# The late part of a four-layer kernel: written order or scheduler's order

## The chip, the cores and the metric

One core of a Trainium2 chip runs the whole program in one launch. Times are device microseconds (us) of an execution. The kernel before was run three times; one more execution was taken with the hardware profiler. A core has five engines that each work through a queue of their own, in the order in which the queue was built: TensorE (PE, with weight loads listed apart as PEld), VectorE (DVE), ScalarE (ACT), GpSimd (POOL) and SyncE (SP, which here only issues DMAs). They wait for each other through semaphores.

## The reference, cut to what matters

Two images of 256 channels and 32 x 32 points pass four residual layers. Layers 0 and 1 are attention over the points; layer 2 is windowed attention and a mixture of experts; layer 3 is additive attention and a mixture of experts. The change concerns what follows layer 2's attention:

```python
t = t + _L2_ffn_ref(_ln_t(t), ...)
t = t + _L3_attn_ref(_ln_t(t), ...)
t = t + _L3_ffn_ref(_ln_t(t), ...)

# _L2_ffn_ref: 8 experts, hidden width 1024; each token uses the best two
h = gelu(einsum('end,edh->enh', xe, W1) + b1)
y = einsum('enh,ehd->end', h, W2) + b2
out = (weights[:, :, None] * sel).sum(axis=1)

# _L3_attn_ref: U = 32 units, a tanh for each pair of points and unit
h = tanh(q[:, :, None, :] + k[:, None, :, :] + bh)
e = einsum('biju,u->bij', h, Wa[:, 0]) + ba[0]
v = einsum('bij,bjd->bid', softmax(e), inputs)

# _L3_ffn_ref: 8 experts, hidden width 512; each token uses the best two
```

All data are float32.

## The kernel before, in words

**The stages.** The late part is a class of generators, one for each stage and image, and each `yield` ends a piece. For an image `b` and a layer `l` (2 or 3):

- `dispatch` (L976 to L1006) normalizes the tokens (`norm`, L939 to L950; `channels`, L952 to L961, turns them by TensorE), chooses experts (`route`), writes each token's row to two places of a table in memory by 16 indirect DMAs of GpSimd (L989), and adds the second bias (transpose, copy to `wT` L1000, matmul L1002).
- `experts` (L1124 to L1226) works through 23 tiles of 128 rows. A tile's weights come by two indirect DMAs on GpSimd's queue (L1140, `up` and `down`, three buffers each), its rows by a DMA on SyncE's (`xr`, L1150). Two transposes turn the rows (L1158). Then follow up matmuls (L1183, two pieces of 8 per tile in layer 2 and one in layer 3), bias on VectorE (L1188), gelu on ScalarE (L1172), down matmuls (L1197, 8 per tile in layer 2 and 4 in layer 3), a copy, and a store on SyncE's queue.
- `collect` (L1228 to L1262) gathers two rows for each token by 16 indirect DMAs (L1241) and adds them, weighted, on VectorE (L1254). For layer 2 it goes on with the norm and with `project` (L1284 to L1307); for layer 3 with `finish` (L1264 to L1280), which writes the output.
- `additive` (L1309 to L1390) is layer 3's attention of one image, in 64 steps. In a step ScalarE makes four tanh tiles of 128 x 1024 (`th`, L1322, eight buffers). A step later `products` puts eight matmuls on TensorE, which pick and sum the units: two halves of 512 keys, and in each half one matmul for every tanh tile, which goes to its own 32 rows of the result, so to its own column group of TensorE:

```python
for a in range(2):
    for c, h in enumerate(tanhs[s]):
        nc.tensor.matmul(
            pe[i][c * U : (c + 1) * U, a, :], lhsT=self.pick[:, k, :], rhs=h[:, a, :],
            start=(k == 0), stop=(k == G - 1),
        )
```

  Eight steps fill one accumulator of 128 x 1024 (`ps_e`, a pool with one buffer, L1331); VectorE copies it out and takes its maximum (L1338). Exponentials (L1349), a turn (L1361) and the values' matmuls (L1368) follow as extra jobs between later steps.

In the profile a matmul of the program shows as two records of TensorE[...]: 1024 products are 2048 records of L1331.

**What sets the order.** `run` (L1393 to L1420) holds a plan: each generator has a start and an end on a common scale and a number of pieces. A heap always advances the generator whose next piece comes first. So the pieces of image 0's attention and of image 1's layer-2 experts alternate, and those of image 1's attention and image 0's layer-3 experts. The program is built in this merged order. In the kernel before, the loop stands inside `with self.tc.manual_schedule():`, under which each engine's queue has its instructions in the order in which the program builds them. Without it, a scheduler places each instruction among those that it takes to be ready, and the order of building gives the priority. Both apply when the program is built, not when it runs.

The pools that limit how far work can run ahead: three buffers each for up weights, down weights and `xr`; two accumulators for the up matmuls; one each for the down matmuls, the turned rows and `ps_e`; two shared by everything else.

Of the kernel before, what the change touches and what calls it, by code (L numbers as in the profile page):

```python
# [858 lines left out]
class Late:  # L859
# [531 lines left out]
    def run(self):  # L1391
        psum = lambda name, bufs: self.ctx.enter_context(self.tc.tile_pool(name=name, bufs=bufs, space=PSUM))
        p_m = psum("lt_m", 2)  # L1393
        self.sb = self.ctx.enter_context(self.tc.tile_pool(name="late_sb", bufs=2))
        self.misc = lambda shape, name: p_m.tile(shape, F32, name=name, tag="ps_m")
        self.p_x, self.p_h, self.p_y, self.p_e = psum("lt_x", 1), psum("lt_h", 2), psum("lt_y", 1), psum("lt_e", 1)

        plan = [
            (self.experts(2, 0), 0, 185, 72),
            (self.dispatch(2, 1), 5, 165, 48),  # L1400
            (self.collect(2, 0), 186, 225, 18),
            (self.experts(2, 1), 186, 480, 72),
            (self.additive(0), 226, 535, 65),
            (self.collect(2, 1), 482, 525, 18),
            (self.additive(1), 536, 850, 65),
            (self.dispatch(3, 0), 546, 622, 40),
            (self.experts(3, 0), 625, 790, 50),
            (self.collect(3, 0), 795, 840, 11),
            (self.dispatch(3, 1), 880, 900, 40),
            (self.experts(3, 1), 905, 1000, 50),  # L1410
            (self.collect(3, 1), 1001, 1040, 11),
        ]
        heap = [(start, k) for k, (_, start, _, _) in enumerate(plan)]
        with self.tc.manual_schedule():
            while heap:
                heap.sort()
                at, k = heap.pop(0)
                step, start, end, pieces = plan[k]
                if next(step, False) is None:
                    heap.append((at + (end - start) / pieces, k))  # L1420


@with_exitstack
# [72 lines left out]
```

## Time and profile before

| | |
|---|---|
| three runs | 3246.14, 3235.66, 3243.29 us |
| median | 3243.29 us |
| profiled execution: its time | 3233.88 us |
| its span | 3232.2 us |
| its mean granted TensorE clock | 0.943 of full |
| instructions | 71102 |
| busy: PE, PEld, DVE, ACT, POOL | 2927.0, 1890.0, 1886.4, 2000.8, 390.9 us |

Stages of the late part in the trace, in us from the span's start:

| event | at |
|---|---|
| layer 2's experts, image 0: first turn, last down | 2024.2, 2258.5 |
| additive attention, image 0: first product, last product | 2325.6, 2668.8 |
| layer 2's experts, image 1: last down | 2594.6 |
| additive attention, image 1: first product, last product | 2680.2, 3005.1 |
| layer 3's experts, image 0: first up, last down | 2771.1, 2942.7 |
| layer 3's experts, image 1: first scatter, first up, last down | 3049.5, 3099.6, 3198.7 |
| end | 3232.2 |

How to read the page: the busy share of an engine is a mean over stages with different limits, so the slices (40 equal parts of the span) and windows of single stretches say more. In a group's row, the first number after the bar is its busy time, the next the mean of one in ns; behind the second bar stands the idle time of the engine just before these instructions, with what ended most of it. In a timeline row stand the start, the length, the engine and line, the operation, how many records, and in brackets the idle time before and its releaser.

### The profile page before, as it was taken

What the parts mean: (1) busy time and instruction counts of PE and PEld (TensorE: products, weight loads), DVE (VectorE), ACT (ScalarE), POOL (GpSimd) and SP (SyncE); (2) the same over time, 40 slices, a digit from 0 to 9 for tenths busy, and PEclk for the clock granted to TensorE, in tenths of its full rate; (3) what the DMA queues carried; (4) which work ended last, traced back from release to release, by engine and by line L of the source; (5) the groups of instructions that cost most, each with busy time, mean ns of one, the idle gap of its engine ahead of it and who ended that gap; (6) DMA issues with size and microseconds to landing.
All of it is one profiled execution on the core that took longest, in us unless ns stands there. A gap on an engine that the chain in (4) does not pass through costs nothing. (4 is left out here: it accounts for less than half of the span.)

```text
span 3232.2 us, 71102 instructions
## 1 busy us (share of the span) xinstructions
PE 2927.0 (91%) x29260; PEld 1890.0 (58%) x29260; DVE 1886.4 (58%) x3668; ACT 2000.8 (62%) x2990; POOL 390.9 (12%) x544
## 2 busy tenths in 40 slices
PE   7999999999999998999999788888699988999565
PEld 4566666666666665566676565776566633564355
DVE  5998898989898986354454574532422243222423
ACT  1887887878788875565566231111399878979200
POOL 3000000000000000000000002232311011322043
PEclk9999999999999998999999887899799998999688
DMA  3000000000000001000000100765554310543066
GB/s 119 3 3 3 3 3 3 3 3 3 3 3 3 3 3 28 1 1 1 1 2 2 24 1 27 269 232 205 208 182 172 134 30 19 175 147 95 19 229 198
DMA packets 175859, 206.85 MB, mean 64 GB/s; under 512 B 118368, under 2 KB 144880, under 8 KB 163760
## 3 DMA queue, kind: packets, MB, share of 16 engines
q0 software_dynamic: 34848, 167.82, 14.8%
q1 hardware_dynamic: 139248, 34.04, 4.8%
q8 instruction: 230, 3.77, 0.5%
q14 instruction: 93, 0.76, 0.1%
q10 hardware_dynamic: 1440, 0.47, 0.1%
HBM read 172.97 MB, written 28.57 MB: 62 GB/s over the span
## 5 line engine op out<-in xcount | busy, mean ns | idle before, releaser
L314 ACT ACTIVATE sc<-sc,sa_shift 128x1024 f32<-128x1024 f32 x512 | 585.1, 1148 | 53.5 <-DMA sa_shift<-sa_min 53.4
L1322 ACT ACTIVATE th<-kT,qb 128x1024 f32<-128x1024 f32 x512 | 541.0, 1134 | 73.7 <-PE ps_e L1331 58.3
L277 PE MATMUL ps_s<-kT,qT 64*32 64x512 f32 x8192 | 504.4, 596 | 9.0 <-ACT sc L287 8.7
L353 PE MATMUL ps_o<-wt,v 128*64 128x128 f32 x6144 | 503.4, 276 | 0.0
L353 PEld LDWEIGHTS ps_o<-wt,v 128*64 128x64 f32 x6144 | 442.2, 137 | 42.6 <-issue 42.6
L327 DVE STREAM_TRANSPOSE wt<-sc 128x768 f32<-128x768 f32 x512 | 465.7, 943 | 1.0 <-ACT sc L314 1.0
L287 ACT COPY sc<-ps_s 128x1024 f32<-128x1024 f32 x256 | 257.4, 1006 | 115.9 <-PE ps_s L277 42.7
L1172 ACT ACTIVATE h<-hb 128x512 f32<-128x512 f32 x138 | 86.1, 624 | 388.0 <-DVE hb L1188 333.8
L1183 PEld LDWEIGHTS ps_h<-xe,ew 128*128 128x128 f32 x2208 | 275.3, 201 | 79.3 <-issue 56.6
L1183 PE MATMUL ps_h<-xe,ew 128*128 128x128 f32 x2208 | 289.9, 288 | 30.4 <-DMA ew<-in_l_up,rt_rows 28.0
L298 DVE TENSOR_REDUCE sa_least<-sc 128x1 f32<-128x1024 f32 x256 | 306.1, 1196 | 1.9 <-ACT sc L287 1.9
L284 DVE TENSOR_SCALAR_CACHE_REDUCE sc<-ps_s 128x1024 f32<-128x1024 f32 x256 | 301.3, 1177 | 5.9 <-PE ps_s L277 5.9
L1331 PE MATMUL ps_e<-th,pick 128*32 128x512 f32 x2048 | 295.2, 616 | 1.4 <-DVE sc_a L1338 1.4
L1197 PE MATMUL ps_y<-ew,h 128*128 128x256 f32 x1104 | 260.6, 386 | 3.9 <-ACT h L1172 2.7
L1188 DVE TENSOR_TENSOR hb<-ps_h,ew 128x512 f32<-128x512 f32 x138 | 95.3, 691 | 280.8 <-PE ps_h L1183 239.2
L154 DVE TENSOR_SCALAR_CACHE_REDUCE sc<-ps_s 128x1024 f32<-128x1024 f32 x128 | 151.8, 1223 | 179.3 <-PE ps_s L148 179.3
L353 PE MATMUL ps_o<-wl,v_odd 128*64 128x128 f32 x2048 | 252.1, 277 | 0.0
L277 PEld LDWEIGHTS ps_s<-kT,qT 64*32 64x32 f32 x8192 | 126.9, 106 | 200.8 <-issue 171.4
L1197 PEld LDWEIGHTS ps_y<-ew,h 128*128 128x128 f32 x1104 | 204.5, 192 | 59.8 <-issue 20.5
L335 PEld LDWEIGHTS ps_t<-ident,sc 128*128 128x128 f32 x1024 | 107.5, 141 | 216.1 <-issue 169.1
L353 PEld LDWEIGHTS ps_o<-wl,v_odd 128*64 128x64 f32 x2048 | 221.3, 137 | 0.0
L335 PE MATMUL ps_t<-ident,sc 128*128 128x128 f32 x1024 | 168.5, 287 | 4.8 <-ACT wl L336 4.1
(269 smaller groups left out, 3607.1 us busy)
## 6 DMA issues: line engine op xcount, KB each, us to landing
xr<-slots_in SPq DMA_DIRECT2D x92, 128.0 KB
slots_out<-y SPq DMA_DIRECT2D x92, 128.0 KB
sa_got<-sa_least SPq DMA_DIRECT2D x512, 0.5 KB
sa_shift<-sa_min SPq DMA_DIRECT2D x512, 0.2 KB
slots_in<-zero POOLq DMA_DIRECT2D x46, 128.0 KB
sa_sums<-sa_total SPq DMA_DIRECT2D x256, 1.0 KB
xT<-in_x SPq DMA_DIRECT2D x4, 496.0 KB
sb_l_w_in<-in_l_w_in SPq DMA_DIRECT2D x1, 1536.0 KB
```

The lines of the kernel that those rows point to most:

```text
L277: nc.tensor.matmul(ps[r][S * c : S * (c + 1), a, :].rearrange("p (b i) -> p b i", i=S), lhsT=qT[half, p, S * i : S * (i + 1)], rhs=keys[ha ...
L284: nc.vector.tensor_scalar(scores[m][0], flat[0], 1.0, None, ALU.mult, ALU.min, accum_out=least[m // 2][:, 0, h : h + 1])
L287: nc.scalar.copy(scores[m][1], flat[1])
L298: nc.vector.tensor_reduce(least[m // 2][:, 1, h : h + 1], scores[m][1], AX.X, ALU.min)
L314: nc.scalar.activation(scores[m][r], scores[m][r], AF.Exp, bias=shift[m // 2][:, r : r + 1], scale=-1.0, accum_out=total[i][:, 2 * p + r, ...
L327: nc.vector.transpose(weights[i, h][:, 2 * p + r, :], scores[m][r][:, :DIRECT])
L335: nc.tensor.transpose(ps[:, g, r, :], s[:, at : at + P], self.ident)
L353: nc.tensor.matmul(sums[i][64 * k : 64 * (k + 1)], lhsT=values, rhs=w, start=(h == 0 and j == 0 and t == 0), stop=(h == 1 and j == 1 and t ...
L1183: nc.tensor.matmul(ps[:, j, :], lhsT=a[:, c, at : at + P], rhs=x[:, c, :], start=(c == 0), stop=(c == CC - 1),)
L1197: nc.tensor.matmul(ps, lhsT=h[:, j, :], rhs=w2[:, j, :], start=(j == 0), stop=(j == HB - 1))
L1322: nc.scalar.activation(h, keys, AF.Tanh, bias=self.qb[b][:, s // G, g : g + 1])
L1331: nc.tensor.matmul(pe[i][c * U : (c + 1) * U, a, :], lhsT=self.pick[:, k, :], rhs=h[:, a, :], start=(k == 0), stop=(k == G - 1),)
```

## The change

The heap loop of `run` leaves the `with` block. The plan, the merged order of building and all stages stay as they are. Layers 0 and 1, whose attention has its own fixed order, are not touched. The whole diff:

```diff
@@ -1411,13 +1411,12 @@
             (self.collect(3, 1), 1001, 1040, 11),
         ]
         heap = [(start, k) for k, (_, start, _, _) in enumerate(plan)]
-        with self.tc.manual_schedule():
-            while heap:
-                heap.sort()
-                at, k = heap.pop(0)
-                step, start, end, pieces = plan[k]
-                if next(step, False) is None:
-                    heap.append((at + (end - start) / pieces, k))
+        while heap:
+            heap.sort()
+            at, k = heap.pop(0)
+            step, start, end, pieces = plan[k]
+            if next(step, False) is None:
+                heap.append((at + (end - start) / pieces, k))
```

Both programs have the same instructions with the same tiles. What differs is their order on the queues: of TensorE's instructions some 8,000 stand elsewhere, of VectorE's some 3,000 rows are involved, and on GpSimd's queue the scatters, gathers and weight fetches are merged in another way.

## The prediction

> **What bounds the kernel now.** I read the slices of the page first, then the windows of the late part (from 2024 us on; the change reaches nothing before it), then the groups, then the order on TensorE and GpSimd inside the stretches that looked full or idle.
>
> ```profile
> PE   7999999999999998999999788888699988999565
> ACT  1887887878788875565566231111399878979200
> PEclk9999999999999998999999887899799998999688
> ```
>
> A slice is 80.8 us. The late part is slices 26 to 40: first TensorE with little ScalarE (image 0's experts), then both full (additive attention beside experts), then a thin tail. The windows put numbers on it: start and end, length, then busy time of PE, weight load, DVE, ACT, POOL, granted clock, DMA share, GB/s.
>
> ```profile
> 2024.00:2260.00 236.00, 198.82 (x1226) 177.25 (x1226) 95.65 (x288) 33.11 (x50) 58.78 (x61) 0.92 0.66 238
> 2260.00:2326.00 66.00, 38.16 (x190) 30.98 (x194) 32.77 (x95) 9.85 (x12) 25.77 (x27) 0.74 0.54 193
> 2380.00:2420.00 40.00, 40.00 (x288) 26.14 (x277) 8.57 (x17) 37.50 (x40) 5.68 (x6) 1.00 0.50 179
> 3005.00:3100.00 95.00, 33.23 (x108) 21.45 (x107) 33.35 (x135) 2.78 (x4) 21.34 (x22) 0.56 0.13 46
> 3100.00:3199.00 99.00, 90.27 (x594) 81.42 (x592) 33.38 (x67) 14.49 (x23) 37.87 (x40) 0.99 0.84 283
> ```
>
> Three kinds of stretch: TensorE with holes (rows 1 and 2: 37 and 28 us idle), TensorE without any (row 3, a sample of 2326 to 2595, where it is busy 268.3 of 269 us), and a tail that waits for scatters (row 4) and then for weights (row 5). In the full stretch ScalarE, which makes the tanhs, is the one that waits, and for the products:
>
> ```profile
> L1322 ACT ACTIVATE th<-kT,qb 128x1024 f32<-128x1024 f32 x512 | 541.0, 1134 | 73.7 <-PE ps_e L1331 58.3
> L1331 PE MATMUL ps_e<-th,pick 128*32 128x512 f32 x2048 | 295.2, 616 | 1.4 <-DVE sc_a L1338 1.4
> ```
>
> So each microsecond added to TensorE between 2326 and 2595 lengthens the kernel by one. TensorE's timeline shows how cheap the products are there:
>
> ```profile
> 2399.55 0.38 PE L1158 MATMUL ps_x<-ident,xr 128*128 128x128 f32 x2
> 2399.86 1.92 PE L1331 MATMUL ps_e<-th,pick 128*32 128x512 f32 x16
> 2401.72 2.05 PE L1183 MATMUL ps_h<-xe,ew 128*128 128x128 f32 x16
> 2403.70 1.93 PE L1331 MATMUL ps_e<-th,pick 128*32 128x512 f32 x16
> ```
>
> A step's eight products (two records each) go to four column groups of 32 and take 1.86 us to the next start. Records of one column group start 0.43 us apart (2399.863, 2400.317, 2400.746, 2401.175), four of them in a row; the other three groups run beside it. Side by side, a product costs 0.23 us; by itself its two records need 2 x 0.43 = 0.86 us before a full-width matmul can follow.
>
> **What the Trainium skill says.** "TensorEngine Tiling (Array Packing)", Key Properties: tiles work independently and in parallel, and a change of tiling mode drains TensorE. The trace agrees with the first (four column groups in the time of one) and doesn't contradict the second: a full matmul starts 0.53 us after the last product record, 0.10 us beyond its 0.43. "DMA: Bandwidth & Descriptors", Two DMAs through the same engine are not ordered: order comes from waiting on the first one's completion. Here each scatter waits for the landing of the one before: in the tail 16 scatters stand 2.67 us apart. "TensorE: Matmul & The Clock Gate", What's actually happening: after an idle window (about 3.4 us) the clock is halved until TensorE has been busy again. The trace agrees: 16 up records take 3.61 us after a hole of 7.34 us and 1.95 us right after.
>
> **The change part by part.** No operation is added or removed. In the built kernel I compared the order on each engine's queue, which executes in order. What moves:
>
> *1. The products are broken up.* Before, all 1024 products stand in unbroken groups of eight or more: 58 runs for image 0, 47 for image 1. After, the scheduler places single products between up and down matmuls, as soon as one tanh is there: 110 runs for image 0 (32 of one, 10 of two, 11 of three, 25 of five, 25 of eight, others) and 91 for image 1. I cost a run at 0.86 us times the products in its fullest column group, plus 0.13 us to leave it and 0.2 us for the extra change of matmul group (an estimate: trace starts of 0.53 against 0.43, and 0.1 to 0.2 where up and down change). A step split 1, 1, 1, 5 costs 0.86 x (1+1+1+2) + 4 x 0.33 = 5.6 us against 2.05. Bounds: streaming alone, 45.6 us for image 0 and 34.4 for image 1 (155.7 and 144.5 against 110.1 each); with 0.6 us instead of 0.33 for each of 52 and 44 extra runs, 77 and 61. Summed along the queue with measured durations (up 0.222 us, down 0.444, turn of x 0.155 per program matmul), first product of image 0 to the last down of image 1's layer-2 experts goes from 272.1 us (trace: 269) to 329.2: **+57**. For image 1 beside layer 3's experts, step 20 to the last down goes from 166.5 (trace 168.3) to 191.9: +25. The rest of image 1's splits lies where ScalarE sets the pace (541.0 us / 512 x 4 = 4.2 us of tanh per step) and is hidden; if not, another 20. On the same queue the first turn of image 0's layer-3 experts stands at product step 17 instead of 19, in front of products that it holds up while the scatters are still running: +5. Sum for image 1: **+30**.
>
> *2. Image 0's layer-2 experts (row 1).* GpSimd's queue (first fence) and TensorE's (second) show the hole; brackets hold the idle time before and what ended it:
>
> ```profile
> 2152.51 1.01 POOL L989 DMA_INDIRECT slots_in<-u,rt_slot  x1 [0.30 <-issue]
> 2160.74 0.99 POOL L989 DMA_INDIRECT slots_in<-u,rt_slot  x1 [7.22 <-DMA slots_in<-u,rt_slot]
> 2162.03 0.99 POOL L1140 DMA_INDIRECT ew<-in_l_down,rt_rows  x1 [0.30 <-issue]
> 2163.33 0.97 POOL L1140 DMA_INDIRECT ew<-in_l_up,rt_rows  x1 [0.30 <-issue]
> ```
>
> ```profile
> 2160.12 3.61 PE L1183 MATMUL ps_h<-xe,ew 128*128 128x128 f32 x16 [7.34 <-DMA ew<-in_l_up,rt_rows]
> ...
> 2171.88 2.02 PE L1183 MATMUL ps_h<-xe,ew 128*128 128x128 f32 x16 [2.69 <-DMA ew<-in_l_up,rt_rows]
> ...
> 2183.20 2.02 PE L1183 MATMUL ps_h<-xe,ew 128*128 128x128 f32 x11 [3.83 <-DMA ew<-in_l_up,rt_rows]
> ```
>
> Scatters for image 1 stand in pairs; the second waits some 7 us for the first, which lands behind two weight fetches, and the next fetches stand behind it. After, scatters and fetches alternate one by one and up goes ahead of down. Waits that can go: for weights 7.3 + 2.7 + 3.8 + 2.3 (two short ones), about 7.5 for the copy of wT ahead of the bias matmul (L1000/L1002, now with up matmuls between), 5.1 for the norm, 1.7 of halved clock: 30. Late next is the weight traffic itself (238 GB/s here, 283 at most seen), so I take three quarters: **-22**, bounds -8 and -33.
>
> *3. The seam (row 2).* Image 1's first up weights stand behind the gathers of collect; TensorE waits 9.8 us for them and 4.8 to 5.5 us three times for norm and turn. After, three fetches of each kind stand before the gathers and four expert tiles before the first product. Of 28 idle us I take **-16** (-8 to -24): collect's own chain of gather, add, norm remains.
>
> *4. The end of image 0's attention.* ScalarE is busy 53 of the 74 us between 2595 and 2669 and the products wait with it for norm and values; norms of both halves move ahead: **-7** (0 to -12).
>
> *5. The tail (rows 4 and 5).* Norm of half 0 of image 1 goes earlier on VectorE, beside the last attention steps: -7.5 of the 44 us before the first scatter. On GpSimd's queue three weight fetches of each kind move ahead of most scatters: they hold the scatters up by about 5, and the first up starts some 3 sooner after the last scatter: +2. Six of 46 fetches are then done when the 99 us stretch begins, whose PE sum is 89: -7.5. On SP's queue the loads of x and the stores of y go with their tiles; no hole of TensorE over 3.7 us ended with them before, so I cost that at nothing, and at 3 us where a load comes late. Sum **-13** (0 to -20). If the cover is gone (norm lands late), it is 0.
>
> Sum: +57 + 30 - 22 - 16 - 7 - 13 = **+29 us** on a span of 3232.2, whose run took 3233.9: 3263. The median of the runs shown, 3243.3, lies 9.4 us above that run; with it 3272. I state 3270.
>
> **The rivals.**
> *The scheduler is right (faster).* One mechanism: TensorE's holes of the late part, 58 us in parts 2 to 5, are filled, and the broken products cost only where their streaming can't hide. For it: the holes are in the profile, and the order names early work for each. Against: in the full stretch nothing hides them, ScalarE already waits. It decides where the broken groups cost under 58 us in all; if a single product takes about 0.6 us instead of 1.19, steps cost half as much more, 87 becomes about 40, and with the holes at 65 the time is 3243 - 25 = 3218.
> *Balance.* Splits at streaming cost alone in the two full stretches, about 60, against 58: 3243.
> *A blocked queue (much slower).* TensorE runs in order; a turn or up placed early in front of ready products waits for scatters or weights. For it: layer 3's first turn stands two steps earlier. With another 40 us of such waits (one tail's worth of 16 scatters at 2.67 us): 3310.
> *The change does nothing* is excluded by the orders, which differ on every queue but ScalarE's, nearly.
>
> **How the numbers follow.** Forecast 0.51 (own range 3255 to 3300), much slower 0.12, balance 0.12, faster 0.25. The measurement can tell about 0.3%, 10 us, from no change; so slower 0.63, same 0.12, faster 0.25. The range 3215 to 3315 leaves out about the lower half of the faster case and a part of the slowest.
>
> **What would show it.** Right: between the first product of image 0 and the last down of image 1's layer-2 experts some 320 us instead of 269, TensorE still full, ScalarE's wait for ps_e well above 58 us, timeline rows of L1331 with x2 records and 0.9 us or more to the next start; the first product near 2288 (2326 less 16 and 22); PE waits for up weights around 2160 gone. Wrong: a lone product that costs 0.5 us or less, or a full stretch under 290 us; or holes of over 5 us in it, for weights, scatters or x, which would be the blocked queue.

## The result, and the profile after

| | before | after |
|---|---|---|
| median (13 runs each) | 3237.79 us | 3250.66 us |
| range | 3232.78 to 3247.16 us | 3243.73 to 3260.64 us |
| span of the profiled execution | 3232.2 us | 3247.5 us |

The ratio is 1.0038, with a 95% interval of [1.0025, 1.0051]: the change costs 0.4%, some 13 us by the medians and 15.3 us by the spans. The forecast had the right sign and its range held the time, but its size, +29 us on the span, was about twice what came. The time that it stated, 3270 us, also rested on the median of three runs of the kernel before, 3243.3; thirteen runs give 3237.8, so 5.5 of the 19 us by which it lies too high come from there.

Behind the small sum stand two large ones. First the slices of the page after:

```profile
PE   7999999999999998999999778998999988999756
ACT  2887888878887884565565321111678878678300
PEclk9999999999999998999999877899999999999778
```

The late part again begins with slice 26. ScalarE is fuller earlier there (the attention starts sooner) and emptier beside the experts. The windows, with the columns as in the prediction, for the same five stages:

```profile
2032.00:2224.00 192.00, 185.78 (x1221) 169.71 (x1222) 83.74 (x249) 33.12 (x50) 63.72 (x66) 0.96 0.89 320
2224.00:2276.00 52.00, 37.06 (x212) 29.65 (x210) 30.03 (x94) 6.38 (x10) 21.93 (x23) 0.87 0.63 212
2380.00:2420.00 40.00, 40.00 (x225) 19.54 (x225) 7.46 (x15) 29.14 (x31) 3.79 (x4) 1.00 0.44 149
3035.00:3125.00 90.00, 30.53 (x104) 20.09 (x103) 24.54 (x104) 2.78 (x4) 21.41 (x22) 0.56 0.19 66
3125.00:3213.00 88.00, 87.34 (x595) 81.98 (x596) 32.60 (x67) 14.48 (x23) 37.94 (x40) 0.98 0.88 303
```

Row 1: image 0's experts take 192 us with TensorE busy for 186; the long holes are gone, the mean granted clock is 0.96 instead of 0.92, and the transfers run at 320 GB/s. Row 3: TensorE is as full as before, but gets through 225 records in 40 us where it got through 288, and ScalarE is busy 29 of 40 us. The groups name the waiting:

```profile
L1322 ACT ACTIVATE th<-kT,qb 128x1024 f32<-128x1024 f32 x512 | 543.0, 1135 | 147.0 <-PE ps_e L1331 135.7
L1331 PE MATMUL ps_e<-th,pick 128*32 128x512 f32 x2048 | 386.1, 608 | 21.0 <-DVE ir_y L935 11.4
```

The same 2048 records of products take 386.1 us of TensorE's time instead of 295.2 although one lasts no longer (608 ns against 616): they overlap less. ScalarE's wait for them is 135.7 us instead of 58.3. TensorE's timeline after shows why:

```profile
2362.99 1.05 PE L1331 MATMUL ps_e<-th,pick 128*32 128x512 f32 x4
2363.97 1.38 PE L1183 MATMUL ps_h<-xe,ew 128*128 128x128 f32 x10
2365.28 1.04 PE L1331 MATMUL ps_e<-th,pick 128*32 128x512 f32 x2
2366.26 0.44 PE L1158 MATMUL ps_x<-ident,xr 128*128 128x128 f32 x2
2366.53 0.83 PE L1183 MATMUL ps_h<-xe,ew 128*128 128x128 f32 x6
2367.30 1.90 PE L1331 MATMUL ps_e<-th,pick 128*32 128x512 f32 x10
```

One product (two records) holds TensorE for 0.98 us until the next start, two products 0.98, five 1.83, eight 1.85. A step in pieces of two, one and five pays 0.98 + 0.98 + 1.83 = 3.79 us where it paid 1.85.

Added up between image 0's first product and the last down of image 1's layer-2 experts, records of products hold TensorE for 145.0 us instead of 95.0, over 103 separate runs instead of 51. The expert matmuls hold it 5.3 us longer, although 26 fewer of their records stand there. Together that is the 55 us by which this stretch grows.

### The profile page after: what moved, and what is told of

Read it like the earlier page. It is cut to its first block, busy times and chain, and to the rows that moved or that the text cites. A ratio compares the mean times of both kernels' runs of the same rounds, so it can differ in the third digit from the quotient of the medians.

```text
span 3247.5 us, 71067 instructions
## 1 busy us (share of the span) xinstructions
PE 2999.5 (92%) x29260; PEld 1886.3 (58%) x29260; DVE 1873.4 (58%) x3668; ACT 2005.1 (62%) x2990; POOL 391.0 (12%) x544
## 4 chain that ended last, share of the span: by engine, by line
PE 85%; DMA 4%; DVE 4%; issue 3%; ACT 2%; POOL 1%; SPq 0%; another core or an unknown queue 0%; ACTq 0%; DVEq 0%; POOLq 0%
PE ps_o L353 15%; PE ps_s L277 15%; PE ps_e L1331 9%; PE ps_h L1183 8%; PE ps_y L1197 7%; PE ps_t L335 4%; PE ps_s L148 4%; PE ps_o L215 4%; PE ps_t L178 3%; DMA slots_in<-u,rt_slot 2%; PE ps_v L1368 2%; PE ps_t L637 2%; PE ps_av L783 1%; PE ps_out L532 1%; PE ps_qk L466 1%
## 5 line engine op out<-in xcount | busy, mean ns | idle before, releaser
L1322 ACT ACTIVATE th<-kT,qb 128x1024 f32<-128x1024 f32 x512 | 543.0, 1135 | 147.0 <-PE ps_e L1331 135.7
L1331 PE MATMUL ps_e<-th,pick 128*32 128x512 f32 x2048 | 386.1, 608 | 21.0 <-DVE ir_y L935 11.4
L1183 PE MATMUL ps_h<-xe,ew 128*128 128x128 f32 x2208 | 296.6, 285 | 13.2 <-DVE t L1254 10.4
L1331 PEld LDWEIGHTS ps_e<-th,pick 128*32 128x32 f32 x2048 | 72.3, 109 | 195.7 <-issue 129.6
```

The source lines that it names most:

```text
L1183: nc.tensor.matmul(ps[:, j, :], lhsT=a[:, c, at : at + P], rhs=x[:, c, :], start=(c == 0), stop=(c == CC - 1),)
L1322: nc.scalar.activation(h, keys, AF.Tanh, bias=self.qb[b][:, s // G, g : g + 1])
L1331: nc.tensor.matmul(pe[i][c * U : (c + 1) * U, a, :], lhsT=self.pick[:, k, :], rhs=h[:, a, :], start=(k == 0), stop=(k == G - 1),)
```

## Where the time went, stage by stage

From the starts and ends of named instructions in the two traces (ends are those of the last record, up to 0.6 us later than in the table of stages before). The stages follow each other without a gap, so the differences sum to the span's:

| stage | before | after | change | forecast |
|---|---|---|---|---|
| to the last down of image 0's layer-2 experts | 2258.9 | 2224.1 | -34.8 | -22 |
| from there to image 0's first product (seam) | 66.7 | 51.9 | -14.8 | -16 |
| from there to the last down of image 1's layer-2 experts | 269.4 | 324.6 | +55.2 | +57 |
| from there to image 0's last product | 74.4 | 71.9 | -2.5 | -7 |
| from there to the last down of layer 3's experts, image 0 | 273.6 | 295.9 | +22.3 | +30 |
| from there to image 1's last product | 62.7 | 66.6 | +3.9 | 0 |
| from there to the last down of image 1's layer-3 experts | 193.4 | 178.4 | -15.0 | -13 |
| to the end | 33.1 | 34.1 | +1.0 | 0 |
| sum | | | +15.3 | +29 |

## The experiments

Medians of the kernel before differ between chips (3229, 3237 and 3227 us in the three groups of runs below), so the time of each kernel (four runs) is read by its ratio to the runs of the kernel before (seven) on its own chip. The stages come from one trace of each kernel; up to the first turn of image 0's layer-2 experts, the traces with the fixed order there differ by up to 5 us among themselves (2023.6 to 2028.4 us), so a difference that small before this point says nothing.

**Whole groups under the scheduler.** In `products`, TensorE's order is fixed within a step, and the column group whose tanh is made last comes first, so all eight products become ready at once:

```diff
-            for a in range(2):
-                for c, h in enumerate(tanhs[s]):
+            with self.tc.manual_schedule(engines={mybir.EngineType.PE}):
+                for a, c in [(a, c) for a in range(2) for c in (3, 0, 1, 2)]:
```

> The changed kernel, with each step's eight products held in a fixed order on TensorE, the one that needs the last tanh first, so that all eight are ready at once; everything else is left to the scheduler. In the built order image 0 has 59 runs of products instead of 110, image 1 has 56 instead of 91. Theory (broken column groups are the loss, the filled holes stay): the stretch from image 0's first product to the last down of image 1's layer-2 experts falls from 325 us to about 271, image 1's stretch from 188 to about 168, and the time is 3251 - 54 - 21, about 3176 us. Rival (the loss comes from the order of the other matmuls, or the early experts' gain is only borrowed from the full stretch): the stretch stays over 310 us, and the time is 3235 to 3250.

Measured: 3157.32 us, ratio 0.9772 [0.9756, 0.9788]. Image 0's stretch beside the experts takes 262.0 us, image 1's 166.3 (from step 20 on), and image 0's experts end as early as in the changed kernel. The window of the stretch in this kernel, with ScalarE's group, and TensorE in the stretch:

```profile
2276.00:2538.00 262.00, 262.00 (x1863) 167.86 (x1862) 61.11 (x123) 244.33 (x256) 31.15 (x33) 1.00 0.45 154
L1322 ACT ACTIVATE th<-kT,qb 128x1024 f32<-128x1024 f32 x512 | 541.1, 1135 | 63.0 <-PE ps_e L1331 59.7
```

```profile
2364.23 1.92 PE L1331 MATMUL ps_e<-th,pick 128*32 128x512 f32 x16
2366.08 1.61 PE L1183 MATMUL ps_h<-xe,ew 128*128 128x128 f32 x12
2367.52 0.38 PE L1158 MATMUL ps_x<-ident,xr 128*128 128x128 f32 x2
2367.74 1.28 PE L1183 MATMUL ps_h<-xe,ew 128*128 128x128 f32 x10
2368.95 1.92 PE L1331 MATMUL ps_e<-th,pick 128*32 128x512 f32 x16
```

Products stand in sixteens of records again, in a stretch that is 63 us shorter, and ScalarE waits 59.7 us for them instead of 135.7. The scheduler still orders everything else, so the rival (the order of the other matmuls, or an early gain only borrowed) falls. The kernel beats both others. Against the kernel before it wins 72 us where 62 were expected; 7 of the difference are the stretch, which came out shorter than with the order of before (262.0 against 269.4): one expert tile fewer stands in it (32 up and 16 down records, 7.1 us), since it was done earlier. The edit does two things, it fixes the order within the step and puts the last tanh's group first. That the second is needed rests on a queue that was built and not run: with the fixed region alone and column groups 0 to 3 as written, it has the same 110 and 91 runs as the changed kernel. No run here separates the two.

**The scheduler for one half only.** The heap loop is cut at plan position 226, where image 0's attention begins; the `with` block stays around one of the halves:

```diff
+        self.advance(heap, plan, 226)
         with self.tc.manual_schedule():
-            while heap:
...
+            self.advance(heap, plan, None)
```

> Only the pieces planned before position 226 (image 0's layer-2 experts, dispatch and collect around them, the first tiles of image 1) are left to the scheduler; from image 0's attention on the order is fixed as before, so all products stand in groups. Theory: the 37 and 15 us that the changed kernel won up to the first product are kept to the end, nothing is lost later: 3238 - 50, about 3188 us, stretch of image 0's attention beside experts about 269. Rival (the early gain is given back later because transfers or the next stage's weights come no sooner): 3220 to 3240.

Measured: 3174.66 us, ratio 0.9826 [0.981, 0.9843]. The first product comes at 2277.9 us instead of 2325.6, the stretch takes 272.5 us, and the lead of 47.7 us has grown to 54.2 at the end. The early gain is real and nothing takes it back.

The other half, with the `with` block around the first call instead:

> The other half: fixed order up to position 226, the scheduler from image 0's attention on. In the built order image 0's products are nearly whole (59 runs), image 1's are broken as in the changed kernel (91 runs). Theory: image 0's stretch 269 to 273 us although the scheduler sets its order, image 1's stretch beside layer 3's experts 188 as in the changed kernel, the turn between the images -9, the tail -15: about 3240 us. Rival (leaving the full stretch to the scheduler costs by itself, broken groups or not): image 0's stretch 300 us or more, time 3270 or more.

Measured: 3243.38 us, ratio 1.0044 [1.0027, 1.006]. Image 0's stretch takes 269.2 us, image 1's 187.6, as expected of whole and of broken groups. So leaving a full stretch to the scheduler costs nothing while the groups happen to stay whole. The median is 14 us above that of before on the same chip, where some 2 were expected. Against the trace of before, from another chip, the span is 7 longer, and by its stages image 1's broken groups (+23.5) outweigh the tail (-15.5). Why image 0's groups stay whole here and break when the early part is left to the scheduler too was not followed up.

**Breaking the groups by hand.** The fixed order of before, with half of each step's products held back until the middle of the next expert piece:

```diff
+            one, two = [[(a, c) for c in range(4)] for a in range(2)]
+            part(one)
+            self.held.append(lambda: part(two))
...
+                if j == 2:
+                    self.flush()
```

> The kernel before with its fixed order, but each step's eight products are held back by half: the four of the first 512 keys, then (inside the next expert piece) the four of the other 512 keys. Each four still go to four different column groups. 171 runs of products in the built order instead of 105. Theory (what costs is the lost side by side, a change of group alone only about 0.18 us): 66 more runs x 0.18, about +12 us, 3250 us. Rival (each break drains TensorE, whatever is in the group; the changed kernel's loss of 77 us over 96 extra runs is 0.8 us each): +53 us, about 3290.

Measured: 3278.43 us, ratio 1.0119 [1.0091, 1.0147], +41 us instead of +12.

For the second kernel `one` and `two` are the column groups 0 and 1, and 2 and 3:

> As the kernel that splits by half, with the same 171 runs, but split by column groups: first both halves of column groups 0 and 1, then both of 2 and 3, so only two groups work side by side. Theory: TensorE's product time by 0.86 us times the fullest column group is 380 us instead of 239; of the 141, the part beside experts (about 45 + 30 split steps x 1.9) sets the time: +110 to +140, about 3365 us. Rival (each break costs the same): as the split by half, both about 3290.

Measured: 3383.61 us, ratio 1.0449 [1.0422, 1.0475], +146 us where +110 to +140 were expected. The two kernels break at the same places, equally often, and differ by 105 us. Timeline rows of the one split by half, then of the one split by columns (four products each):

```profile
2401.97 1.06 PE L1335 MATMUL ps_e<-th,pick 128*32 128x512 f32 x8
2402.97 1.99 PE L1201 MATMUL ps_y<-ew,h 128*128 128x256 f32 x8
```

```profile
2403.15 1.91 PE L1335 MATMUL ps_e<-th,pick 128*32 128x512 f32 x8
2404.99 1.16 PE L1185 MATMUL ps_h<-xe,ew 128*128 128x128 f32 x8
```

Four products over four column groups hold TensorE for 1.00 us, over two groups for 1.84. So a break by itself costs 2 x 1.00 - 1.85 = 0.15 us in the products, and two things more around them: 0.09 for the extra change into products (0.205 us from an up matmul's start to a product's, against 0.112 to another up matmul), and 0.10 for the first up or down record after products (0.213 us to the next start against 0.112, 0.320 against 0.216, the same in the traces of before, after and both splits). The fence of the restored groups shows both: twelve up records after products hold TensorE for 1.44 us, where twelve times 0.112 would be 1.34, and ten ahead of products for 1.21, where it would be 1.12. That makes 0.34 us for a break with nothing lost side by side; the rest of what a split costs is lost work side by side.

The full stretch beside image 1's layer-2 experts has 45 breaks more than before in both kernels. For the split by half they make 45 x 0.34 = 15.3 us, and the stretch grows by 14.6; for the split by columns 45 x (2 x 1.84 - 1.85 + 0.19) = 90.9 us, and it grows by 90.7. The rival, a drain that each break pays whatever is in the group, falls. My +12 for the split by half was too low: it took 66 breaks at 0.18 us, and the whole trace has 73 at 0.34, about 25 us of the 41. The rest is not in the breaks: from the last expert piece to the last product the two attentions take 6.3 and 6.2 us longer, with no break more, and ScalarE idles 7.8 and 4.8 us longer there ahead of its tanhs. That the held products free their tanh tiles later would explain this, but no run of its own shows it.

**The early hole.** Three kernels with the fixed order of before. First only the weight fetches move:

```diff
-            fetch(m + 2, 1)
             fetch(m + 3, 0)
             inputs(m + 3)
...
+            fetch(m + 2, 1)
             down(m)
```

> The kernel before with its fixed order, only the place of the weight fetches changed: up weights are fetched as soon as the up matmuls have read the buffer, down weights just ahead of the down matmuls, so that GpSimd's queue has scatters and fetches one by one. Theory (the early hole is weights behind paired scatters): image 0's layer-2 experts take 200 to 210 us instead of 234, layer 3's last experts some 5 us less: about 3205 us. Rival (most of the early gain comes from the norm and bias waits, or from work moved ahead): 225 us or more, time 3225 or more.

Measured: 3211.0 us, ratio 0.9948 [0.9928, 0.9969]. Image 0's experts end at 2242.3 us instead of 2258.9: 17 us, between the theory and its rival. The queue is not one by one throughout: three times two scatters still stand in a row, and the second waits 3.6 to 6.3 us. The two kernels that follow keep such pairs.

Then the transpose for the second bias goes a tile ahead as well:

```diff
+            if i < IT:
+                nc.tensor.transpose(ps, p[:, i, :], self.ident)
...
+            i, ps = i - 1, self.misc([P, C], "ps_b2")
```

> The kernel with the moved weight fetches, and in dispatch the transpose for the second bias goes one tile ahead of its matmul, so that TensorE doesn't stand for the copy of wT. In the run with moved fetches alone, image 0's layer-2 experts still took 219 us against 192 of the changed kernel, and eight waits for wT there sum to 8.0 us. Theory (what is left of the early hole is TensorE waiting for norm and bias copies): another -8 in that stage, 211 us, about 3203 us. Rival (what is left is weight traffic, and a wait removed is waited again at the next weights): 217 us or more, 3209 to 3213.

Measured: 3200.31 us, ratio 0.9915 [0.989, 0.9941]. From the first to the last down the stage takes 198.3 us instead of 200.9: the eight waits for wT are gone, but only 3 of their 8 us are won there. The rival is right about this stage: 5 us are waited again, for down weights. The kernel gains elsewhere: the time from image 0's last product to the last down of layer 3's experts falls by 8.6 us, and layer 3's dispatch has the same bias step.

Last, a piece boundary between norm and its transposes (a `yield` ahead of `self.channels` in `normed`):

> As the one before, and one more piece boundary between the normalizing on VectorE and the transposes of its result on TensorE, so that an expert piece stands between. Two such waits of image 1's dispatch sum to 3.4 us in the run with moved fetches (1.19 and 2.17), and in the seam two of 5.5. Theory: -3 in image 0's experts, up to -8 in the seam: about 3195 us. Rival (the pieces that get between are short, or the seam's wait is for weights): within 3 us of the run before it.

Measured: 3184.2 us, ratio 0.9873 [0.9851, 0.9895]. From first to last down the stage takes 192.5 us, 5.8 less where 3 were expected, and the seam 63.2 instead of 65.1, 1.9 less where up to 8 were expected. The first product comes 15 us sooner than in the run before it, but 4 of these lie ahead of the stage, where nothing was changed. TensorE's longest remaining waits in the stage are for weights alone:

```profile
2154.50 3.69 PE L1203 MATMUL ps_y<-ew,h 128*128 128x256 f32 x16 [2.75 <-DMA ew<-in_l_down,rt_rows]
2166.16 5.38 PE L1203 MATMUL ps_y<-ew,h 128*128 128x256 f32 x16 [4.07 <-DMA ew<-in_l_down,rt_rows]
2178.08 3.69 PE L1203 MATMUL ps_y<-ew,h 128*128 128x256 f32 x16 [1.91 <-DMA ew<-in_l_down,rt_rows]
2189.34 5.38 PE L1203 MATMUL ps_y<-ew,h 128*128 128x256 f32 x16 [2.11 <-DMA ew<-in_l_down,rt_rows]
```

With 0.76 for up weights these make 11.6 us, about the 12.7 by which the changed kernel is still ahead (179.8 us from first to last down, with 2.2 us of waits for weights). The changed kernel's GpSimd queue in the same place, and the longest wait for weights that TensorE has left there:

```profile
2149.70 0.99 POOL L989 DMA_INDIRECT slots_in<-u,rt_slot  x1 [2.69 <-DMA slots_in<-u,rt_slot]
2150.99 0.97 POOL L1140 DMA_INDIRECT ew<-in_l_up,rt_rows  x1 [0.30 <-issue]
2153.93 0.99 POOL L989 DMA_INDIRECT slots_in<-u,rt_slot  x1 [1.97 <-DMA slots_in<-u,rt_slot]
2155.23 0.97 POOL L1140 DMA_INDIRECT ew<-in_l_down,rt_rows  x1 [0.30 <-PE ps_h L1183]
```

```profile
2169.33 1.13 PE L1183 MATMUL ps_h<-xe,ew 128*128 128x128 f32 x8 [1.78 <-DMA ew<-in_l_up,rt_rows]
```

Here no two scatters stand in a row while both kinds are on the queue. A scatter with one fetch ahead of it waits 1.3 to 4.1 us, not 7. That the pairs left in the fixed order make the rest of the difference is likely, but no run without them was made.

## Why the prediction was right in sign and wrong in size

**Right: what bounds the kernel.** The full stretch has no hole before or after, and what TensorE gains or loses there is the kernel's: +55.2 against +57.

**Right: the mechanism of the loss.** Column groups that no longer work side by side: shown from both sides, by the kernel that restores the groups (the loss goes) and by the two that break them (the loss comes, and follows the fullest column group). Its price was right too. I put a run's fixed cost at 0.33 us; it is 0.31, of which 0.12 to leave (0.98 - 0.86), 0.10 at the first record after it and 0.09 to enter. A lone product costs 1.17 us; I had 1.19. Of the +55.2, 52 extra runs at 0.31 make 16 us, the 26 expert records that stand elsewhere take off 4, and some 43 are work no longer done side by side, where streaming alone was forecast at 45.6.

**Wrong: the size of part 2.** This is the step that failed: "Late next is the weight traffic itself (238 GB/s here, 283 at most seen), so I take three quarters: **-22**, bounds -8 and -33." The stage won 34.8 us, beyond even the bound. Two steps of that sum failed.

- *The quarter taken off for weight traffic.* I had listed 28.7 us of waits. From first to last down, TensorE's idle time falls from 31.3 to 3.0 us, so nearly all of it went. The rate that I took for a limit, 283 GB/s, was only the most that I had seen: in the changed kernel the stage moves some 5 MB more (61 instead of 56, by the two windows) at 320 GB/s, and TensorE is busy 186 of 192 us.
- *The halved clock, put at 1.7 us.* I priced it after one hole. Between first and last down TensorE's granted clock stood at half for 27.3 us before and for 3.4 after (means of 0.94 and 0.99), and the busy time there falls by 8.9 us, although 32 more up records stand in it. An estimate from these figures: half of the 23.9 us, some 12, is the most that the clock can account for, had TensorE worked all through them.

The first down comes 2.3 us later than before, which takes these 37 us back to 34.8. In the fixed order, waits for norm and bias that were taken away one after the other came back in part as waits for weights, and with fetches, bias and norm all moved 12.7 us were still missing. This term is 12.8 of the 13.7 us between forecast and result.

**Wrong: image 1's attention.** +22.3 instead of +30. From step 20 to the last down the queue sum gave +25 and +21.6 came. Products hold TensorE for 77.7 us instead of 56.5, and all its work there takes 24.2 us more, as forecast; but 2.6 us in which it had stood idle went, and the sum along the queue knows no idle time. The 5 us for layer 3's first turn that blocks ready products did not come: it waits 6.8 us for its rows, but image 1's step 20 is only 0.6 us later after image 0's last product.

**Small terms.** Seam and tail came within 2 us. The end of image 0's attention gave 2.5 instead of 7, the end of image 1's, which I had at nothing, cost 3.9; the latter was not traced to a cause. All the terms but part 2 together miss by 0.9 us, but that is luck: their errors have both signs (-7.7 and -2.0, +4.5 and +3.9 the largest).

**What the Trainium skill told.** Its page "TensorEngine Tiling (Array Packing)", Key Properties, has tiles working independently: the measured 1.00 us for four products in four groups, against 1.84 in two, agrees. The drain on a change of mode that it names can be at most part of the 0.31 us of leaving and entering measured here.

**The rivals.** "The scheduler is right" failed at its own decision point: the holes were worth 67 us (34.8 + 14.8 + 2.5 + 15.0), more than its 58, but the broken groups cost over 77. "A blocked queue" is not in the trace of the full stretch, where TensorE never waits.

## What to carry to other kernels

When matmuls on separate column groups work side by side, keep their pack together on the queue: fix the order within the pack and put first the one whose input comes last, so that a scheduler that places what is ready finds all of them ready at once; here these two together turned a loss of 0.4% into a gain of 2.3%. When a hole in one stage has several waits in a row, a transfer rate seen while the queue was waiting is no limit: ask what the rate is with the queue unblocked, expect a single repair to show less than the wait that it removes, and count what the holes do to the clock of the work after them. A change whose sum is near nothing can hold two large terms of opposite sign: split it by stage before calling it neutral, since each half may be had without the other.

## What the runs showed of the hardware that was not expected

- Products of 32 columns: one alone holds TensorE for 0.98 us, four in four column groups for 1.00 us, five for 1.83, eight for 1.85.
- The first up or down record after products takes 0.10 us longer to the next start than those that follow (0.213 against 0.112, 0.320 against 0.216), whatever number of products went before.
- Indirect weight fetches that alternated strictly with scatters on one GpSimd queue ran at 320 GB/s over 192 us. With two fetches and two scatters in turn the stage ran at 238, and with fetches moved but three pairs of scatters left at 257. That the alternation alone sets the rate is not shown: the changed kernel also has five more fetches in the stage.
